# Second batch's gates, gating and out_proj placed between two layers; in_proj's weights and features split into parts

## The chip, the cores and the metric

The program runs on one core of one Trainium2 chip. The metric is device time in microseconds (us) of one execution, with all weights and activations starting in HBM. Six executions of the kernel before have a median of 670.97 us (669.88 to 676.37). One execution was profiled; it took 670.53 us, of which the profile's span covers 668.8 us.

Engine names: PE is TensorE's matmul stream (PEld its weight loads), DVE is VectorE, ACT is ScalarE, POOL is GpSimd, SP is SyncE, which here only issues DMAs. "L573" is line 573 of the kernel.

## The reference

Two fused layers on x of shape (2, 512, 256), all in fp32. Layer 0 adds to the input the product of two branches; layer 1 the same with other branches.

```
xn = layernorm(x)
s  = mamba2(xn)            # rms norm, in_proj, conv, chunked scan, silu gate, out_proj, + xn
g  = silu(moe(xn))         # 8 experts of width 704, the best 2 of each token
x  = x + s * g
xn = layernorm(x)
s  = attention(xn)         # 32 query heads, 8 key/value heads of 64, rotary, causal
g  = silu(signed_ffn(xn))  # layernorm, sign, product with the signs of the centred weights
x  = x + s * g
```

What the change touches is the end of the first branch. With `z, ssm, B, C, dt` the parts of `h @ in_proj_w` (z is the first 512 columns):

```
y_ssd = scan(conv(ssm), B, C, dt) + D * conv(ssm)
y_ssd = y_ssd * silu(z)
s     = xn + y_ssd @ out_proj_w
```

## The kernel before, in words

Tokens are cut in 8 tiles of 128 (`NT`), four per batch (`TPB`); 256 channels are `KC` = 2 contraction steps of 128. An fp32 matmul appears in the trace as two records.

**Front.** SP loads x, the small parameters and in_proj's weights `w_in` (L206, 2 DMAs). Both batches are normalised, transposed and put in `hT` (features on partitions; one tile for both batches) and `xT` (for the router). `gates(b)` (L376) computes four heads of `silu(z)` into `gT[b]` and then B and C into `BC`: each is two matmuls of 128x512 (`features`, L370). `gates(0)`, the token-major B and dt columns (L402), the router (L243 to L356), the discretisation `dt`, `la`, `cum` (L413 to L439), `convolved(0, h)` for four heads (L384) and `gates(1)` (L449) follow in the program. A framework orders each engine's instructions here by its own cost model; the result is one fixed queue per engine, executed in order.

**Experts and scan.** The mixture of experts runs as 19 blocks of 128 rows (`blocks`, `hidden` L573, `project` L588). A block's tokens and weights come by indirect DMAs on POOL (L549), its rows go back by one (L592) to the DRAM tensor `chosen`. Between the blocks stand the scan's chunks, `chunk(b, i0)` = `decays`, `outputs`, `gated`, `scanned` (L540): `gated` (L520) adds D * ssm on DVE and multiplies by `gT`; `scanned` (L532) is out_proj, four matmuls of 128x256 (L536), and the addition of `xn` into `s0` (L538). Chunks (0,0) to (0,3), (1,0) and (1,1) are complete there; of (1,2) and (1,3) only `decays`. `early_weights` (L627) loads keys' and values' weights in one tile `w_kv` (in the memory of `hT`), the rotary tables and layer 1's signed weights.

**The turn between the layers** (L907 to L932) is written in a fixed order (`manual_schedule`): SP issues the fetch of batch 0's expert rows from `chosen` (`fetched`, L681: two DMAs into `xn`, two into `y1`), then queries' weights `w_q` (2 x 1 MB), then `outputs`, `gated`, `scanned` of chunks (1,2) and (1,3). `activated` adds the two experts' rows on POOL (L694) and applies silu on ACT (L695); `residual` (L697) makes x1 and its statistics on DVE; `normed1` and `features1` normalise and transpose into `x1T`. Then come the first key, query and two value projections. `fetched(1)` overwrites `xn` rows of batch 1, so each of its DMAs must follow the `scanned` that reads those rows.

**Attention** (from L939) uses eight PSUM banks taken over from the earlier pools; its first scores (L829) can't start before the last use of the old banks, the two copies of values `v` on ACT (L780), is done. Batch 1's residual, norm and features are spread over its first steps (`others`).

Of the kernel before, what the change touches and what calls it, by code (L numbers as in the profile page):

```python
# [8 lines left out]
F32 = mybir.dt.float32  # L9
# [33 lines left out]
def fused_kernel(  # L43
# [33 lines left out]
    def bank_a():  # L77
        return psum.tile([P, 512], F32, tag="A", name="bank_a")

    def bank_b():  # L80
        return psum.tile([P, 512], F32, tag="B", name="bank_b")
# [21 lines left out]
    def par(name):  # L103
        a, w = SM[name]
        return sm[:, a : a + w]
# [66 lines left out]
    def rsqrt(var, scale, eps, name):  # L172
        return rooted(root(var, eps, name))
# [12 lines left out]
    def normed(dst, src, b, mv, r, eng=V):  # L186
        for i in range(TPB):
            t = b * TPB + i
            eng.tensor_scalar(dst[:, t, :], src[:, t, :], mv[:, i, 0:1], r[:, i : i + 1],
                              ALU.subtract, ALU.mult)  # L190
# [10 lines left out]
    def batch(b):  # L201
        return slice(b * T, (b + 1) * T)

    w_in = mem.tile([P, KC, in_w.shape[1]], F32, tag="w_in", name="w_in")
    for k in range(KC):
        nc.sync.dma_start(w_in[:, k, :], in_w[k * P : (k + 1) * P, :])  # L206
    w_out = mem.tile([P, NH, C], F32, tag="w_out", name="w_out")


# [2 lines left out]
    xn = mem.tile([P, NT, C], F32, tag="xn", name="xn")  # L212
    xT = mem.tile([P, KC, B * T], F32, tag="xT", name="xT")
    hn = mem.tile([P, NT, C], F32, tag="s0", name="hn")
    hT = mem.tile([P, KC, B * T], F32, tag="hT", name="hT")
    norms = []
    for b in range(B):
        mv, var, r = statistics(x_sb, b, "ln0")
        ms = stat.tile([P, TPB], F32, tag="ms", name=f"ms{b}")
        V.tensor_tensor(ms, r, r, ALU.mult)  # L220
        V.tensor_tensor(ms, ms, var, ALU.mult)
        rr = rsqrt(ms, 1.0, 1e-6, f"rms{b}")
        V.tensor_tensor(rr, rr, r, ALU.mult)
        norms.append((mv, r))
        normed(hn, x_sb, b, mv, rr, (V, G)[b])
        to_features(hn, b, lambda k, ps: S.mul(
            hT[:, k, batch(b)], ps, par("norm")[:, k : k + 1]))
    for b in range(B):
        normed(xn, x_sb, b, *norms[b])
        for t in range(b * TPB, (b + 1) * TPB):  # L230
# [138 lines left out]

    def features(b, col, ps):  # L370
        for k in range(KC):
            PE.matmul(ps, lhsT=w_in[:, k, col : col + P], rhs=hT[:, k, b * T : (b + 1) * T],  # L372
                      start=(k == 0), stop=(k == KC - 1))
        return ps

    def gates(b):  # L376
        for h in range(NH):
            ps = features(b, h * P, bank_a())
            S.activation(gT[b][:, h, :], ps, AF.Silu)
        for n, col in enumerate((o_b, o_c)):  # L380
            ps = features(b, col, bank_a())
            S.copy(BC[:, n, batch(b)], ps)

    def convolved(b, h):  # L384
        ps = features(b, DI + h * P, bank_b())
# [13 lines left out]
    for t in range(NT):  # L399
        ps = bank_b()  # L400
        for k in range(KC):
            PE.matmul(ps[:, : NH + P], lhsT=hT[:, k, t * P : (t + 1) * P],  # L402
                      rhs=w_in[:, k, o_dt : o_dt + NH + P],
                      start=(k == 0), stop=(k == KC - 1))
        V.tensor_tensor(dtr[:, t, :], ps[:, :NH], par("dtb"), ALU.add)
        S.copy(Btok[:, t, :], ps[:, NH : NH + P])
# [34 lines left out]
    def heads(ap):  # L441
        return ap.rearrange("p (h n) -> p h n", h=NH)

    def wide(name, t):
        return mw.tile([P, NH, P], F32, tag=name, name=f"{name}{t}")

    for h in range(NH):
        convolved(0, h)
    gates(1)  # L449


    states, parts = [None] * B, {}
# [64 lines left out]
                PE.matmul(y, lhsT=state[:, h, :], rhs=cs[:, h, :], start=False, stop=True)  # L517
        parts[t] = yps

    def gated(b, i0):  # L520

        t = b * TPB + i0
        ti = slice(i0 * P, (i0 + 1) * P)
        yps = parts[t]
        yg = wide("yg", t)
        for h in range(NH):
            V.scalar_tensor_tensor(yg[:, h, :], ssmT[b][:, h, ti], par("D")[:, h : h + 1],
                                   heads(yps)[:, h, :], ALU.mult, ALU.add)
        V.tensor_tensor(yg, yg, gT[b][:, :, ti], ALU.mult)
        parts[t] = yg  # L530

    def scanned(b, i0):  # L532
        t = b * TPB + i0
        ops = bank_b()
        for h in range(NH):
            PE.matmul(ops[:, :C], lhsT=parts[t][:, h, :], rhs=w_out[:, h, :],  # L536
                      start=(h == 0), stop=(h == NH - 1))
        V.tensor_tensor(s0[:, t, :], ops[:, :C], xn[:, t, :], ALU.add)  # L538

    def chunk(b, i0):  # L540
        for part in (decays, outputs, gated, scanned):
            part(b, i0)


# [80 lines left out]


    def early_weights():  # L627
        w_kv = mem.tile([P, 2, KC, KV * HD], F32, tag="hT", name="w_kv")
        nc.sync.dma_start(w_kv[:, 0], wk.rearrange("(k p) n -> p k n", p=P))
        nc.sync.dma_start(w_kv[:, 1], wv.rearrange("(k p) n -> p k n", p=P))  # L630
        rw = mem.tile([P, 2 * T + KC * C], F32, tag="w_in", name="rw")
        nc.sync.dma_start(rw[:, : 2 * T].rearrange("p (n t) -> p n t", n=2), rope)
        nc.sync.dma_start(rw[:, 2 * T :].rearrange("p (o c) -> p o c", o=KC),
                          ffn_w.rearrange("(o p) c -> p o c", p=P))
        return (w_kv, rw[:, : 2 * T].rearrange("p (n t) -> p n t", n=2),
                rw[:, 2 * T :].rearrange("p (o c) -> p o c", o=KC))


# [12 lines left out]
    convolved(1, 2)  # L651
    blocks(2)
    convolved(1, 3)
    w_kv, cs_t, w_f = early_weights()
    blocks(3)
    chunk(1, 0)
    blocks(5)
# [23 lines left out]
    def fetched(b):  # L681

        y1 = aw.tile([P, TPB, C], F32, tag=f"pr{b}", name=f"y1_{b}")
        by_tile = chosen.rearrange("(s p) c -> p s c", p=P)
        for t in range(b * TPB, (b + 1) * TPB, 2):
            nc.sync.dma_start(xn[:, t : t + 2, :], by_tile[:, t : t + 2, :])
            nc.sync.dma_start(y1[:, t % TPB : t % TPB + 2, :], by_tile[:, NT + t : NT + t + 2, :])
        return y1

    def activated(b, y1):  # L690

        for i in range(TPB):
            y = xn[:, b * TPB + i, :]
            G.tensor_tensor(y, y, y1[:, i, :], ALU.add)  # L694
            S.activation(y, y, AF.Silu)  # L695
# [10 lines left out]
    def means(b):  # L706
        return stat.tile([P, TPB, 2], F32, tag="mv", name=f"ln1_mv{b}")
# [1 line left out]
    x1T = mem.tile([P, KC, B * T], F32, tag="xT", name="x1T")  # L709

    def normed1(b, mv):
        var = stat.tile([P, TPB], F32, tag="var", name=f"ln1_var{b}")
        V.tensor_copy(var, mv[:, :, 1])
        normed(xn, x1, b, mv, rsqrt(var, 1.0, 1e-5, f"ln1{b}"))

    def features1(b):
        to_features(xn, b, lambda k, ps: S.copy(x1T[:, k, batch(b)], ps))
# [30 lines left out]
    def rotated(dst, ps, scale, name, between=None):  # L748

        sw = aw.tile([P, T], F32, tag="sw", name=f"sw_{name}")  # L750
        V.stream_shuffle(sw, ps, swap)
        V.scalar_tensor_tensor(dst, ps, scale, cs_t[:, 0, :], ALU.mult, ALU.mult)
        if between:
            between()
        V.scalar_tensor_tensor(sw, sw, scale, cs_t[:, 1, :], ALU.mult, ALU.mult)
        V.tensor_tensor(dst, dst, sw, ALU.add)

    def projected(w, n, b):
        ps = bank()
        for k in range(KC):  # L760
            PE.matmul(ps, lhsT=w[:, k, n * P : (n + 1) * P], rhs=x1T[:, k, batch(b)],  # L761
                      start=(k == 0), stop=(k == KC - 1))
        return ps

    kT, v_sb = {}, {}

    def key(b, m):
        if m == 0:
            kT[b] = mem.tile([P, KV // 2, T], F32, tag=f"gT{b}", name=f"kT{b}")
        rotated(kT[b][:, m, :], projected(w_kv[:, 0], m, b), HD**-0.5, f"k{b}_{m}")  # L770

    def value(b, i):
        if i == 0:
            v_sb[b] = mem.tile([P, TPB, KV * HD], F32, tag=f"ssmT{b}", name=f"v{b}")
        t = b * TPB + i
        ps = bank()
        for k in range(KC):
            PE.matmul(ps, lhsT=x1T[:, k, t * P : (t + 1) * P], rhs=w_kv[:, 1, k, :],  # L778
                      start=(k == 0), stop=(k == KC - 1))
        S.copy(v_sb[b][:, i, :], ps)  # L780

# [125 lines left out]
    with tc.manual_schedule():  # L907
        y1s = [fetched(0)]
        query_weights(0)
        query_weights(1)  # L910
        outputs(1, 2)
        gated(1, 2)
        outputs(1, 3)
        gated(1, 3)
        scanned(1, 2)

        activated(0, y1s[0])
        mvs = [means(0)]
        for t in range(2):
            residual(t, mvs[0])  # L920
        scanned(1, 3)
        y1s.append(fetched(1))
        for t in range(2, TPB):
            residual(t, mvs[0])
        normed1(0, mvs[0])
        features1(0)
        activated(1, y1s[1])
        key(0, 0)
        nextq = query(0, 0)
        for i in range(2):  # L930
            value(0, i)
        mvs.append(means(1))  # L932
# [249 lines left out]
```

## Time and profile before

| what | us |
|---|---|
| median of 6 executions | 670.97 |
| the profiled execution, whole | 670.53 |
| its span | 668.8 |
| PE busy | 624.2 |
| DVE busy | 438.3 |
| ACT busy | 376.4 |
| POOL busy | 287.9 |
| the chunks' out_proj (L536), one chunk on the chain | 1.73 to 1.76 |
| w_q (2 x 1 MB), issue to landing, median | 11.1 |
| xn and y from `chosen` (256 KB), issue to landing, medians | 3.8 and 4.0 |
| w_kv from in_wv (512 KB), issue to landing | 6.4 |

The page divides the span by engine, by 40 slices, by DMA queue, and by the chain of waits that ends with the last instruction. Busy shares are averages over stages; the stages themselves are read from tables of stretches (busy time of each engine and the TensorE clock granted, 1.00 being full speed) and from the timeline, which merges like instructions of an engine and tells, in brackets, the idle time before them and what ended it.

### The profile page before, as it was taken

The page shows a single profiled execution, that of the slowest core. Times are in us where ns is not written, and L with a number is a line of the kernel's source. Part 1 is how long each engine was busy: PE and PEld are TensorE (multiplying, and loading weights), DVE is VectorE, ACT ScalarE, POOL GpSimd, SP SyncE. Part 2 cuts the span into 40 slices and gives each one's busy share as a digit, 9 for nine tenths or more (in the row PEclk, how much of TensorE's full clock was granted, in tenths as well). Part 3 has the DMA queues.
Part 4 walks back from the last instruction along what each step waited for, and adds up shares of the span by engine and source line. Part 5 has one row for each costly group of instructions (what it writes and reads, how often), then busy time and mean ns, then how long its engine had stood idle before and what let it go on. Part 6 is the DMA issues. An engine that isn't in the chain of part 4 may idle for free.

```text
span 668.8 us, 11923 instructions
## 1 busy us (share of the span) xinstructions
PE 624.2 (93%) x4260; PEld 447.8 (67%) x4260; DVE 438.3 (66%) x1453; ACT 376.4 (56%) x948; POOL 287.9 (43%) x308
## 2 busy tenths in 40 slices
PE   1899999999999998499889999989999999999997
PEld 0564988889999987245545565546886666665676
DVE  7186856642522453689989996999228888888511
ACT  3345625522312240476888985968308988888710
POOL 2221433234455321336555746454305666677600
PEclk9999999999999999699999999999999999999999
DMA  7042140353445402500000000021000000000000
GB/s 244 9 189 95 33 152 17 131 192 120 165 159 171 151 9 80 188 1 1 1 1 1 1 1 1 2 68 60 8 25 1 1 1 1 1 2 1 1 1 32
DMA packets 17804, 38.83 MB, mean 58 GB/s; under 512 B 4845, under 2 KB 12783, under 8 KB 16592
## 3 DMA queue, kind: packets, MB, share of 16 engines
q0 software_dynamic: 7296, 24.66, 10.7%
q1 hardware_dynamic: 10448, 13.40, 6.1%
q8 instruction: 34, 0.56, 0.4%
q14 instruction: 26, 0.21, 0.1%
HBM read 56.13 MB, written 4.59 MB: 91 GB/s over the span
## 4 chain that ended last, share of the span: by engine, by line
PE 72%; DVE 17%; issue 5%; POOL 2%; DMA 2%; ACT 1%; SPq 0%; POOLq 0%; DVEq 0%
PE bank_a L573 11%; PE bank L880 9%; PE bank L888 8%; PE bank L868 7%; PE bank L761 7%; PE bank L829 7%; PE bank_a L588 6%; DVE pr L842 4%; PE bank_a L372 2%; PE bank_b L536 2%; DMA chosen<-o,dest 1%; PE bank_b L372 1%; PE bank L778 1%; PE bank L740 1%; DVE cv L394 1%
## 5 line engine op out<-in xcount | busy, mean ns | idle before, releaser
L856 POOL TENSOR_SCALAR pr<-pr,den 128x128 f32<-128x128 f32 (+2 forms) x192 | 193.4, 1023 | 159.3 <-DVE den L1039 126.1
L848 ACT ACTIVATE pr<-pr,nmax 128x128 f32<-128x128 f32 (+3 forms) x256 | 142.8, 559 | 18.6 <-DVE nmax L842 17.2
L842 DVE CUSTOM_DVE_ANT_0 pr<-bank,cmask 128x128 f32<-128x128 f32 (+3 forms) x256 | 109.8, 484 | 14.8 <-PE bank L829 14.5
L573 PEld LDWEIGHTS bank_a<-xgT,w 128*128 128x128 f32 x836 | 97.2, 192 | 2.2 <-DVE xgT L562 0.7
L573 PE MATMUL bank_a<-xgT,w 128*128 128x128 f32 x836 | 97.9, 275 | 0.5 <-DVE xgT L562 0.5
L869 ACT COPY pt<-bank 128x384 f32<-128x384 f32 (+1 forms) x192 | 85.0, 519 | 13.1 <-PE bank L868 13.1
L868 PEld LDWEIGHTS bank<-ident,pr 128*128 128x128 f32 x640 | 71.2, 141 | 24.8 <-issue 18.3
L880 PE MATMUL bank<-pt,v 128*64 128x256 f32 (+3 forms) x512 | 82.9, 443 | 0.8 <-ACT pt L869 0.8
L868 PE MATMUL bank<-ident,pr 128*128 128x128 f32 x640 | 75.7, 273 | 6.0 <-DVE oT L1023 5.7
L880 PEld LDWEIGHTS bank<-pt,v 128*64 128x64 f32 x512 | 39.2, 136 | 49.1 <-ACT pt L869 23.3
L829 PE MATMUL bank<-kT,q 64*64 64x128 f32 (+7 forms) x1024 | 69.8, 410 | 0.7 <-ACT v L780 0.7
L761 PE MATMUL bank<-x1T,w_q 128*128 128x512 f32 x124 | 61.5, 618 | 0.0
L888 PE MATMUL bank<-w_o,oT 128*128 128x256 f32 x256 | 56.1, 380 | 0.6 <-DVE oT L1020 0.6
L888 PEld LDWEIGHTS bank<-w_o,oT 128*128 128x128 f32 x256 | 48.3, 190 | 7.7 <-DVE oT L1020 0.8
L588 PE MATMUL bank_a<-wp,hid 128*128 128x256 f32 x228 | 53.4, 380 | 0.1
L549 POOL DMA_INDIRECT w<-in_moe_w,wrow x19 | 20.3, 1071 | 70.3 <-PE bank_a L560 45.8
L848 ACT ACTIVATION_READ_ACCUMULATOR pr<-pr,nmax 128x1 f32 x256 | 49.1, 192 | 0.0
L829 PEld LDWEIGHTS bank<-kT,q 64*64 64x64 f32 x1024 | 38.0, 133 | 14.3 <-issue 5.1
L577 DVE TENSOR_TENSOR hid<-hid,bank_a 128x512 f32<-128x512 f32 x19 | 13.0, 686 | 51.8 <-issue 36.6
L761 PEld LDWEIGHTS bank<-x1T,w_q 128*128 128x128 f32 x124 | 21.0, 189 | 36.9 <-issue 27.7
L588 PEld LDWEIGHTS bank_a<-wp,hid 128*128 128x128 f32 x228 | 41.4, 190 | 5.0 <-DVE hid L577 0.3
L854 ACT ACTIVATE pr<-pr,den 128x512 f32<-128x512 f32 x32 | 23.1, 723 | 22.7 <-DVE den L1061 22.7
(250 smaller groups left out, 851.7 us busy)
## 6 DMA issues: line engine op xcount, KB each, us to landing
w_q<-in_wq SPq DMA_DIRECT2D x2, 1024.0 KB, 11.1
w_o<-in_wo SPq DMA_DIRECT2D x2, 1024.0 KB, 7.2
w_in<-in_in_w SPq DMA_DIRECT2D x2, 642.0 KB, 5.9
x_sb<-in_x SPq DMA_DIRECT2D x8, 128.0 KB, 2.5
rows<-xn SPq DMA_DIRECT2D x8, 128.0 KB, 2.7
xn<-chosen SPq DMA_DIRECT2D x4, 256.0 KB, 3.8
y<-chosen SPq DMA_DIRECT2D x4, 256.0 KB, 4.0
out_x<-y SPq DMA_DIRECT2D x8, 128.0 KB, 1.7
```

What stands on the lines that cost most here:

```text
L573: PE.matmul(banks[bank][:, i * P : (i + 1) * P], lhsT=w[:, a : a + P], rhs=xgT[:, k * P : (k + 1) * P], start=(k == 0), stop=(k == KC - 1))
L588: PE.matmul(ps[:, :C], lhsT=hid[:, j * P : (j + 1) * P], rhs=wp[:, j * C : (j + 1) * C], start=(j == 0), stop=(j == 5))
L761: PE.matmul(ps, lhsT=w[:, k, n * P : (n + 1) * P], rhs=x1T[:, k, batch(b)], start=(k == 0), stop=(k == KC - 1))
L829: PE.matmul(pss[hh][to, a : a + full], lhsT=q[half, n * HD : (n + 1) * HD], rhs=kT[b][half, m, :full], start=True, stop=True)
L842: V.tensor_tensor_reduce(w["pr"][hh][:, span(i)], w["ps"][i][hh], cmask[:, i & 1, T - (i + 1) * P :], -1.0, 3.0e38, ALU.add, ALU.min, w["n ...
L848: S.activation(x, x, AF.Exp, scale=-1.0, bias=w["nmax"][hh][:, i : i + 1], accum_out=sum_of(w, i, hh))
L854: S.mul(x, x, sum_of(w, i, hh))
L856: eng.tensor_scalar(x, x, sum_of(w, i, hh), None, ALU.mult)
L868: PE.transpose(ps[:, col : col + P], pr[hh][:, at : at + P], ident)
L869: S.copy(pts[hh][:, bank_at[n] : bank_at[n] + widths[n]], ps[:, : widths[n]])
L880: PE.matmul(pv[hh * HD : (hh + 1) * HD, j * P :], lhsT=v_sb[b][:, j, g * HD : (g + 1) * HD], rhs=pts[hh][:, at : at + w], start=(j == 0), ...
L888: PE.matmul(ps[:, :C], lhsT=oTs[b][:, c, i * P : (i + 1) * P], rhs=made["w_o"][c // 8][:, c % 8, :], start=(c == 0), stop=(c == PAIRS - 1))
```

## The change

1. `w_in` is two tiles: `w_z` (the 512 columns of z) and `w_in` (the other 772), loaded by 2 + 2 DMAs. `hT` is two tiles, one for each batch.
2. `gates` takes a list of parts. In the front, `gates(1, ...)` computes only B and C. The four heads of z of batch 1 are computed in the turn.
3. `gated` is split in `passed` (D * ssm + y) and `gated` (the product with `gT`), `scanned` in `projected_out` (matmuls) and `scanned` (addition). Batch 0's chunks do all in place; batch 1's do only `passed` there, into a new tile `held` for all four chunks (in the memory of `xT`).
4. In the turn: `outputs` and `passed` of chunks (1,2), (1,3); for each head the gate's two matmuls, silu, and one product of 128x512 over all four chunks; the load of values' weights `w_v`, issued by ACT into the memory of batch 1's `hT`; `activated(0)`; four `projected_out`; four `residual`; `normed1(0)`; four `scanned`; only then `fetched(1)`.
5. `early_weights` loads keys' weights `w_k` alone, into batch 0's `hT`. The fetch of batch 0's `y1` is issued by ACT in place of SP; that of batch 1 stays with SP.
6. `normed1` reads the variances in place, without a copy.

```diff
-    w_in = mem.tile([P, KC, in_w.shape[1]], F32, tag="w_in", name="w_in")
+    w_z = mem.tile([P, KC, DI], F32, tag="w_z", name="w_z")
+    w_in = mem.tile([P, KC, in_w.shape[1] - DI], F32, tag="w_in", name="w_in")
...
-    hT = mem.tile([P, KC, B * T], F32, tag="hT", name="hT")
+    hT = [mem.tile([P, KC, T], F32, tag=f"hT{b}", name=f"hT{b}") for b in range(B)]
...
-    gates(1)
+    gates(1, range(NH, NH + 2))
...
+    def passed(b, i0):
+        t = b * TPB + i0
+        ti = slice(i0 * P, (i0 + 1) * P)
+        if b and not held:
+            held.append(mem.tile([P, NH, T], F32, tag="xT", name="held"))
+        yg = held[0][:, :, ti] if b else wide("yg", t)
+        for h in range(NH):
+            V.scalar_tensor_tensor(yg[:, h, :], ssmT[b][:, h, ti], par("D")[:, h : h + 1],
+                                   heads(parts[t])[:, h, :], ALU.mult, ALU.add)
+        parts[t] = yg
+
+    def gated(b, i0):
+        yg = parts[b * TPB + i0]
+        V.tensor_tensor(yg, yg, gT[b][:, :, i0 * P : (i0 + 1) * P], ALU.mult)
+
+    def projected_out(b, i0):
+        ops = bank_b()
+        for h in range(NH):
+            PE.matmul(ops[:, :C], lhsT=parts[b * TPB + i0][:, h, :], rhs=w_out[:, h, :],
+                      start=(h == 0), stop=(h == NH - 1))
+        parts[b * TPB + i0] = ops
 
     def scanned(b, i0):
         t = b * TPB + i0
-        ops = bank_b()
...
-        V.tensor_tensor(s0[:, t, :], ops[:, :C], xn[:, t, :], ALU.add)
+        V.tensor_tensor(s0[:, t, :], parts[t][:, :C], xn[:, t, :], ALU.add)
 
     def chunk(b, i0):
-        for part in (decays, outputs, gated, scanned):
+        for part in (decays, outputs, passed) + ((gated, projected_out, scanned) if b == 0 else ()):
             part(b, i0)
...
-            nc.sync.dma_start(y1[:, t % TPB : t % TPB + 2, :], by_tile[:, NT + t : NT + t + 2, :])
+            (nc.sync if b else nc.scalar).dma_start(y1[:, t % TPB : t % TPB + 2, :], by_tile[:, NT + t : NT + t + 2, :])
...
-        outputs(1, 2)
-        gated(1, 2)
-        outputs(1, 3)
-        gated(1, 3)
-        scanned(1, 2)
+        for i0 in (2, 3):
+            outputs(1, i0)
+            passed(1, i0)
+        for h in range(NH):
+            gates(1, (h,))
+            V.tensor_tensor(held[0][:, h, :], held[0][:, h, :], gT[1][:, h, :], ALU.mult)
+        w_v = mem.tile([P, KC, KV * HD], F32, tag="hT1", name="w_v")
+        nc.scalar.dma_start(w_v, wv.rearrange("(k p) n -> p k n", p=P))
+        late_weights.append(w_v)
 
         activated(0, y1s[0])
+        for i0 in range(TPB):
+            projected_out(1, i0)
         mvs = [means(0)]
-        for t in range(2):
-            residual(t, mvs[0])
-        scanned(1, 3)
-        y1s.append(fetched(1))
-        for t in range(2, TPB):
+        for t in range(TPB):
             residual(t, mvs[0])
         normed1(0, mvs[0])
+        for i0 in range(TPB):
+            scanned(1, i0)
+        y1s.append(fetched(1))
         features1(0)
```

## The prediction

> **What bounds the kernel now.** I read first the table of stretches, to see where PE is full. Columns: busy time (and instructions) of PE, PEld, DVE, ACT, POOL, then the granted clock, the DMA share and GB/s.
>
> ```profile
> 26.00:66.00 40.00, 39.95 (x171) 23.74 (x169) 26.61 (x118) 18.18 (x33) 6.43 (x6) 1.00 0.32 119
> 66.00:135.00 69.00, 67.37 (x440) 58.12 (x440) 45.67 (x113) 34.67 (x50) 23.93 (x22) 1.00 0.25 85
> 135.00:200.00 65.00, 65.00 (x473) 60.59 (x472) 24.37 (x55) 17.18 (x32) 29.12 (x29) 1.00 0.47 158
> ...
> 258.00:277.00 19.00, 7.74 (x49) 6.42 (x47) 12.89 (x40) 3.16 (x6) 4.03 (x5) 0.82 0.68 223
> ```
>
> Until 258 us PE has no gap worth naming; in the turn it has 11.3 us of them. So PE work taken out of a full stage pays if nothing else ends that stage, and is free in the turn if PE isn't what ends the turn. Next, what ends the turn, from the chain of waits (start, us, what):
>
> ```profile
> 257.92 4.48 DMA chosen<-o,dest
> ...
> 263.40 3.52 DMA y<-chosen
> ...
> 277.19 2.26 PE bank_a L197 x8
> ```
>
> The last expert block's rows go to DRAM, come back, and run through POOL, ACT and DVE until PE transposes them at 277.19. From there to the first scores, the timeline:
>
> ```profile
> 265.86 0.51 SPq L686 DMA_DIRECT2D xn<-chosen  x1
> ...
> 277.94 2.93 POOL L694 TENSOR_TENSOR xn<-xn,y 128x256 f32<-128x256 f32 x4 [7.72 <-DMA y<-chosen]
> ...
> 286.98 0.59 ACT L780 COPY v<-bank_b 128x512 f32<-128x512 f32 x1 [1.13 <-PE bank_b L778]
> 287.62 2.38 PE L829 MATMUL bank<-kT,q 64*64 64x128 f32 x32 [0.68 <-ACT v L780]
> ```
>
> The scores wait for the second copy of v on ACT. Ahead of that copy in ACT's queue stand batch 1's four silus, fed by POOL, fed by `fetched(1)`. Last, the places that the change empties:
>
> ```profile
> 50.47 6.17 PE L372 MATMUL bank_a<-hT,w_in 128*128 128x512 f32 x14
> 56.48 0.30 PE L437 MATMUL bank_b<-la,upper 128*128 128x32 f32 x2
> 56.62 7.11 PE L372 MATMUL bank_b<-hT,w_in 128*128 128x512 f32 x16
> ```
> ```profile
> 56.01 0.19 DVE L433 SCALAR_TENSOR_TENSOR la<-dt,ab 128x32 f32<-128x32 f32 x1
> ```
> ```profile
> 181.35 1.76 PE bank_b L536 x8
> ...
> 225.88 1.76 PE bank_b L536 x8
> ```
>
> Batch 1's gates run from 50.47 to 56.6 while DVE makes `la`, which is ready at 56.2: they fill a wait.
>
> **Front: 6.9 us of PE out, 2.0 gained.** Four heads at two matmuls of two records, 16 x 0.43 = 6.9 us. The compiled order of the changed kernel on PE tells what takes their place: after the last B/dt matmul (50.6) come three transposes of expert tokens, then `la`'s matmul (L437 before), then the convolutions. PE executes in order, so convolutions that need nothing from `la` stand behind it until 56.2, as ACT's and DVE's instructions for `la` are the same as before. PE thus idles 56.2 - 50.6 - 0.3 (transposes) = 5.3 us. The convolutions start within 0.2 us of the old time, and so does their chain (ACT copy, four DVE operations, silu: about 3.6 us a head). Behind them PE saves the last gate record pair (0.9), the transposes done early (0.3) and two waits it had (0.36 before L482, 0.48 before L573), and starts the first block's `hidden` near 64.8 instead of 67.38. Following the new DVE order by these durations, its fourth head is ready near 77.4, when PE has come to it: new waits of about 0.4. Sum: 6.9 - 5.3 - 0.4 + 0.8 = 2.0. It can't exceed 6.9 - 5.3 + 1.5 = 3.1 (all waits of that stage gone, 67.37 of 69 being busy).
>
> No row shows a gap of 5.6 us holding three transposes. The clock rows bound it:
>
> ```profile
> 270.00:270.50 0.50, 0.00 (x0) 0.00 (x0) 0.47 (x3) 0.25 (x1) 0.22 (x1) 0.66 0.91 213
> ...
> 280.00:280.50 0.50, 0.50 (x2) 0.21 (x1) 0.00 (x0) 0.48 (x2) 0.50 (x2) 0.60 0.00 0
> ```
>
> PE stopped at 265.9, the clock halved 4.3 us later (0.66 is the mean of the slice), and came back 3.1 us after work began at 277.19. A drop in the front would cost half of 3.1, 1.55, leaving 0.45. The longest stretch without any matmul is about 2.5 us (53.7 to 56.2), nearer to the gaps that cost nothing (the 4.3 before the drop), so I take no drop, and keep 0.45 as the other end.
>
> [...]
>
> **Blocks: 3.5 us.** `projected_out` of chunks (1,0) and (1,1) leaves a stage with PE 65.00 of 65.00 and 40.00 of 40.00: 2 x 1.76 = 3.5. What could be late next is a block's weights, but blocks without a chunk already run every 7.7 us without a PE wait, and those with one still take longer (2.59 of L588, 4.91 of L573, 0.2 of transposes and the chunk's remaining 2 to 3 us). DVE's two 0.69 products there cost nothing, being covered by PE.
>
> **Turn: 0.9 us longer**, on the old clock, from the same last scatter (257.92).
> - PE: `outputs` end at 261.9; gates 6.9, to 268.8; 16 out_proj matmuls (4 x 1.73 = 6.9) follow, the first 13 from 268.8 on as products arrive, done near 276.5. This fits in the 11.3 us gap; without it, 10.4 us would be on the path.
> - ACT: y1's two issues (0.4 to 0.5 each, by SP's rows) before the first silu is due at 263.6; last silu 269.4; w_v's issue, to 269.9 (its memory is free with the gates' last matmul; its 512 KB, 6.4 us by in_wv's row, are due at 283.4). Behind it stand the four silus of `activated(0)`, which began at 267.84: now 269.9, after POOL has long added.
> - DVE: four products of 0.69, paced by silu, the last to 270.1; `residual(0)` at 270.35 instead of 268.29. Four at 1.47 (271.99 to 273.46), without the old `scanned` and the slow first one (L701 0.83 against 0.43): 276.2. Root and norm 1.45 as before (L713's 0.2 is gone): transposes at 278.2, 1.0 later.
> - PE no longer cools, so the 1.55 of half clock after 277.19 is saved; values end near 286.9, as before (286.96).
> - `scanned` x4 (0.42) follow `normed1` on DVE: 279.1 to 280.8. `fetched(1)`, before at 265.86 and 272.10, now issues at 280.0 to 281.3; SP has nothing else to do until w_o's load much later. With 3.52 to land, POOL adds from 283.9 (4 x 0.73) to 286.9, ACT's last silu ends at 287.3, two copies of v at 288.45 against 287.58: +0.9. Ends: landing in 2.5 (x_sb's row) gives -0.1, since then PE's values end it; 5.4 (272.50 to 277.94) gives +2.7. I take 3.52, a fetch ahead of other traffic.
>
> **Nothing for the rest.** Two more issues on SP at 6.45 (0.48 each) end before its next job at 9.37. w_k moves from 147.93 to about 64, when the DMA share is 0.02; if it met block weights, 512 KB at the 270 to 430 GB/s that loaded stretches show would delay them 1.2 to 1.9 us. `held` takes the memory of xT, free since the router.
>
> Sum: -2.0 - 3.5 + 0.9 = -4.6 on the profiled execution: 670.53 - 4.6 = 665.9. The median shown lies 0.44 above that execution, so 666.4 for a median.
>
> **Rivals.**
> - *The clock drops in the front*: 666.4 + 1.55 = 667.9. For: idle 5.6 against 4.3. Against: transposes break it.
> - *The front gives nothing and the turn takes its upper end*: -3.5 + 2.7 + 0.44 on 670.53, 670.2. For: DVE's convolution chain is serial and now has the expert work between its steps. Against: DVE is busy 45.67 of 69 there.
> - *All moved PE work pays*: 6.9 + 3.5 - 0.9 = 9.5, 661.5. Only if PE didn't stand behind `la`; the compiled order says it does.
> - *The fetch of batch 0 is held behind w_q* (the slower side). SP now issues w_q right after two xn fetches, while y1 comes from ACT. For: the fetch issued behind w_q at 265.86 and 266.41 reached POOL only at 277.94, 11.5 us. If y1 lands with w_q, near 275, the first silu is at 275.9, `residual(0)` at 276.3 instead of 270.35: +6.0, 672.4; with POOL's pacing and the clock drop 674.5. It decides once y1 lands after 269.2. Against: y1 and w_q wait for the same event at 262.5, so y1 is issued no later.
>
> [...]
>
> **How the numbers follow.** Forecast 0.50, clock drop 0.23, nothing from the front 0.12, all pays 0.05, y1 held 0.10. Range: from 664.2 (forecast with 3.1 in the front and -0.1 in the turn, 664.3) to 669.4, which covers the drop (667.9) with most of the turn's upper end; outside are "all pays", "y1 held" and part of the third. A measurement of this kernel can tell about 0.5% from no change, 3.35 us: below 667.6 is faster, above 674.3 slower. Faster: 0.44 of the forecast's 0.50, 0.08 of the drop, 0.05: 0.57. Slower: 0.07, mostly from y1. Same: 0.36.
>
> **What would show it.** Right: PE idle from about 50.7 to 56.2 with `la`'s matmul at its end; the chain of the blocks' end 5 to 6 us earlier; no drop of the clock in the turn; scores about 30.5 us after the last scatter's issue (29.7 before), waiting for v's copies on ACT. Wrong: `hidden` of the first block not before 66; clock 0.5 near 57; POOL's first add later than 11 us after the last scatter.

## The result, and the profile after

The changed kernel takes 675.09 us (median of 35 runs, 673.71 to 678.08); the kernel before, run beside it, 672.22. The ratio is 1.0043 with a 95% interval of 1.0034 to 1.0053: slower by some 2.9 us, where 4.6 us of gain were forecast, and outside the range given. The execution profiled took 673.78 us, with a span of 672.1 (before 668.8); it is one of the fastest, 1.3 us below the median, and no execution of it on record was granted a higher clock than its 0.990.

Four marks split the span. "Forecast" is the mark that the prediction's own steps give for the profiled execution.

| mark, us | before | forecast | after |
|---|---|---|---|
| first block's `hidden` starts on PE | 67.38 | 64.8 | 67.80 |
| last scatter to `chosen` issued | 257.92 | 252.4 | 260.27 |
| first scores | 287.62 | 283.0 | 291.27 |
| end of span | 668.8 | 664.2 | 672.1 |

So, for the profiled execution, 3.0 us are missing by the first block, 4.9 more in the blocks and 0.4 in the turn; what follows takes as long as before (380.8 us from the scores on, 381.2 before). The table of stretches of the changed kernel shows the first two places. The columns are stretch, length, busy time (and instructions) of PE, PEld, DVE, ACT, POOL, then the granted clock, the DMA share and GB/s.

```profile
26.00:66.00 40.00, 35.00 (x150) 21.23 (x149) 24.21 (x114) 15.65 (x29) 7.44 (x7) 0.91 0.34 122
66.00:135.00 69.00, 64.25 (x416) 55.71 (x415) 46.48 (x111) 36.38 (x50) 20.93 (x19) 0.98 0.24 80
135.00:200.00 65.00, 65.00 (x461) 59.60 (x460) 24.40 (x56) 18.16 (x32) 28.57 (x28) 1.00 0.45 150
...
57.00:62.00 5.00, 5.00 (x7) 2.18 (x8) 1.85 (x5) 0.59 (x1) 0.00 (x0) 0.50 0.08 32
129.70:134.00 4.30, 4.30 (x16) 3.78 (x17) 1.38 (x5) 0.51 (x2) 0.13 (x1) 0.60 0.82 328
...
281.00:285.00 4.00, 4.00 (x12) 2.43 (x12) 1.97 (x6) 1.24 (x3) 0.00 (x0) 0.63 0.41 127
```

PE now has 5.0 us of gaps in 26 to 66 and 4.75 in 66 to 135 (0.05 and 1.63 before). In three places PE works at half clock, each right behind a gap. The timeline of the front (start, length, engine, line, operation; in brackets the idle time before it and what ended it):

```profile
53.02 0.44 PE L577 MATMUL bank_a<-ident,xg 128*128 128x128 f32 x2 [2.14 <-DMA xg<-rows,tok]
55.07 0.33 PE L577 MATMUL bank_a<-ident,xg 128*128 128x128 f32 x1 [1.61 <-DMA xg<-rows,tok]
56.60 0.61 PE L443 MATMUL bank_b<-la,upper 128*128 128x32 f32 x2 [1.20 <-DVE la L439]
57.02 9.65 PE L377 MATMUL bank_b<-hT,w_in 128*128 128x512 f32 x16
```

PE idles 2.14 + 1.61 + 1.20 = 4.95 us until `la`, as forecast (5.3). But the 16 records of the convolutions take 9.65 us in place of 7.11: 2.5 us lost to the clock (0.50 in 57 to 62). In finer slices the half clock reaches from 55.3 to 62.1.

The second place, in the timeline around the two waits of the blocks (L605 is `project`, L594 the product that makes `hid`, L476 to L496 the scan's `decays`):

```profile
108.95 0.38 PE L577 MATMUL bank_a<-ident,xg 128*128 128x128 f32 x2
109.04 0.86 DVE L476 SCALAR_TENSOR_TENSOR L<-bank_b,cum,negm 128x128 f32<-128x128 f32 x3
...
109.82 0.15 DVE L480 TENSOR_TENSOR dte<-bank_b,cum 128x4 f32<-128x4 f32 x1
109.89 0.68 DVE L496 TENSOR_TENSOR cs<-BC,ec 128x512 f32<-128x512 f32 x1
110.48 0.68 DVE L594 TENSOR_TENSOR hid<-hid,bank_a 128x512 f32<-128x512 f32 x1
...
111.27 1.10 PE L605 MATMUL bank_a<-wp,hid 128*128 128x256 f32 x4 [1.93 <-issue]
...
127.43 0.86 DVE L476 SCALAR_TENSOR_TENSOR L<-bank_b,cum,negm 128x128 f32<-128x128 f32 x3
...
128.27 0.69 DVE L496 TENSOR_TENSOR cs<-BC,ec 128x512 f32<-128x512 f32 x1
...
128.87 0.69 DVE L594 TENSOR_TENSOR hid<-hid,bank_a 128x512 f32<-128x512 f32 x1
...
129.66 0.67 PE L605 MATMUL bank_a<-wp,hid 128*128 128x256 f32 x2 [2.83 <-issue]
```

DVE has no gap in either. It works through five operations of the next chunk's `decays` (L476 three times, L480 and L496), and only then makes the product for which PE stands still. ACT isn't what the product waits for: the silu that it reads (L593) was done at 101.7 and 119.2. At the same place the kernel before had put a chunk's `outputs` between the block's `hidden` and its `project`, and PE waited 0.69 us (the same view of before):

```profile
108.61 0.38 PE L560 MATMUL bank_a<-ident,xg 128*128 128x128 f32 x2
...
109.69 1.12 PE L502 MATMUL bank_b<-xe,Btok 128*128 128x512 f32 x2 [0.69 <-DVE xe L492]
...
110.35 0.69 DVE L577 TENSOR_TENSOR hid<-hid,bank_a 128x512 f32<-128x512 f32 x1 [0.38 <-ACT hid L576]
...
112.43 0.81 PE L588 MATMUL bank_a<-wp,hid 128*128 128x256 f32 x3
```

The turn after, from the chain of waits (start, us, what); its lines of before stand in the prediction:

```profile
264.25 6.88 PE bank_a L377 x16
271.15 0.41 ACT gT L385
...
272.40 0.43 DVE xn L716
...
280.78 2.25 PE bank_a L197 x8
...
290.26 0.97 ACT v L794 x2
291.27 2.38 PE bank L843 x32
```

The gates, the last silu and four residuals now set the transposes at 280.78, 20.5 us after the last scatter (issued at 260.27; 19.3 before); the scores follow it by 31.0 (29.7 before, 30.6 forecast). What they wait for is what was forecast, the copies of v behind batch 1's silus on ACT; POOL stood idle for 1.28 us before its second pair of additions for them (at 288.40), and the last silu ended 30.0 us after the scatter, where 29.4 were worked out.

### The profile page after: what moved, and what is told of

Same layout as the page of the kernel before. It is cut to its first block, busy times and chain, and to the rows that moved or that the text cites. A ratio compares the mean times of both kernels' runs of the same rounds, so it can differ in the third digit from the quotient of the medians.

```text
span 672.1 us, 11934 instructions
## 1 busy us (share of the span) xinstructions
PE 628.4 (94%) x4260; PEld 450.2 (67%) x4260; DVE 439.2 (65%) x1452; ACT 379.7 (56%) x950; POOL 288.3 (43%) x308
## 4 chain that ended last, share of the span: by engine, by line
PE 44%; DVE 14%; issue 1%; POOL 1%; ACT 0%; DVEq 0%; POOLq 0%; ACTq 0%
PE bank L894 9%; PE bank L902 8%; PE bank L882 7%; PE bank L775 7%; PE bank L843 7%; DVE pr L856 4%; PE bank L792 1%; PE bank L754 1%; PE bank_a L377 1%; DVE sw_q L765 1%; DVE xn L189 1%; DVE q L766 1%; POOL pr L870 1%; DVE oT L1042 1%; DVE oT L1039 1%
## 5 line engine op out<-in xcount | busy, mean ns | idle before, releaser
L856 DVE CUSTOM_DVE_ANT_0 pr<-bank,cmask 128x128 f32<-128x128 f32 (+3 forms) x256 | 109.9, 485 | 14.2 <-PE bank L843 14.1
L894 PE MATMUL bank<-pt,v 128*64 128x128 f32 (+3 forms) x512 | 82.9, 443 | 0.8 <-ACT pt L883 0.8
L605 PE MATMUL bank_a<-wp,hid 128*128 128x256 f32 x228 | 54.6, 386 | 4.8 <-issue 4.8
L902 PE MATMUL bank<-w_o,oT 128*128 128x256 f32 x256 | 56.1, 380 | 0.6 <-DVE oT L1039 0.6
L605 PEld LDWEIGHTS bank_a<-wp,hid 128*128 128x128 f32 x228 | 41.9, 193 | 10.0 <-issue 5.2
L594 DVE TENSOR_TENSOR hid<-hid,bank_a 128x512 f32<-128x512 f32 x19 | 13.1, 687 | 52.7 <-issue 36.6
```

Of the source, the lines that this page charges most:

```text
L605: PE.matmul(ps[:, :C], lhsT=hid[:, j * P : (j + 1) * P], rhs=wp[:, j * C : (j + 1) * C], start=(j == 0), stop=(j == 5))
L856: V.tensor_tensor_reduce(w["pr"][hh][:, span(i)], w["ps"][i][hh], cmask[:, i & 1, T - (i + 1) * P :], -1.0, 3.0e38, ALU.add, ALU.min, w["n ...
L894: PE.matmul(pv[hh * HD : (hh + 1) * HD, j * P :], lhsT=v_sb[b][:, j, g * HD : (g + 1) * HD], rhs=pts[hh][:, at : at + w], start=(j == 0), ...
L902: PE.matmul(ps[:, :C], lhsT=oTs[b][:, c, i * P : (i + 1) * P], rhs=made["w_o"][c // 8][:, c % 8, :], start=(c == 0), stop=(c == PAIRS - 1))
```

## The experiments

All twelve, in one table; the marks are those of each profiled execution.

| run | median us | ratio to before, 95% | last scatter | scores |
|---|---|---|---|---|
| changed kernel | 675.09 | 1.0043 (1.0034 to 1.0053) | 260.27 | 291.27 |
| e1_gates_front | 668.54 | 0.9942 (0.9922 to 0.9962) | 254.68 | 284.93 |
| e2_hid_first | 669.06 | 0.9952 (0.9932 to 0.9972) | 255.53 | 287.38 |
| e3_conv_first | 667.55 | 0.9917 (0.9891 to 0.9944) | 254.00 | 285.73 |
| e4_conv_hid | 663.07 | 0.9850 (0.9825 to 0.9875) | 251.77 | 283.11 |
| e5_filler | 671.97 | 0.9992 (0.9974 to 1.0009) | 258.14 | 289.31 |
| e6_wq_late | 663.30 | 0.9865 (0.9843 to 0.9886) | 248.22 | 280.55 |
| e7_turn | 661.10 | 0.9832 (0.9809 to 0.9854) | 248.66 | 278.49 |
| e8_before_hid | 674.44 | 1.0043 (1.0020 to 1.0067) | 260.25 | 291.40 |
| e9_filler2 | 674.75 | 1.0036 (1.0024 to 1.0048) | 260.65 | 292.18 |
| e10_before_conv_hid | 673.83 | 1.0026 (1.0010 to 1.0041) | 260.17 | 291.55 |
| e11_filler_hid | 667.19 | 0.9927 (0.9906 to 0.9949) | 253.38 | 285.42 |
| e12_turn_only | 672.91 | 1.0006 (0.9990 to 1.0022) | 261.48 | 292.42 |

**e1: one part undone.** In the changed kernel, batch 1's z gates go back to the front.

```diff
-    gates(1, range(NH, NH + 2))
+    gates(1)
...
-            gates(1, (h,))
```

> The changed kernel with one part undone: the four z heads of batch 1 are computed in the front again (gates(1) whole), and the turn only multiplies. Its compiled order in front and blocks is that of the kernel before, less the two out_proj. Theory (the loss sits in the order of the fixed queues: PE idle ahead of la's matmul with a half clock behind it, and two waits of 1.93 and 2.83 us ahead of project's matmuls with another half clock): hidden of the first block starts near 67.4, no wait ahead of project, the last scatter is issued near 257.9 - 3.5 = 254.4, no half clock before the turn; time 672.2 - 3.5 + 0 to 1.3 for the turn = 668.7 to 670.0. Rival (taking out_proj out of the blocks frees nothing, or the split of weights and features costs time by itself): last scatter near 257.9 or later, 672 to 674.

The stretch of the blocks' first part, and the last scatter in the timeline:

```profile
66.00:135.00 69.00, 67.37 (x441) 57.99 (x440) 45.88 (x115) 34.77 (x49) 23.85 (x22) 1.00 0.26 89
```
```profile
254.68 0.98 POOL L609 DMA_INDIRECT chosen<-o,dest  x1 [6.50 <-ACTq L686]
```

Measured: `hidden` at 67.67, no wait ahead of `project`, the last scatter at 254.68 (3.24 before that of the kernel before), 668.54 us. The out_proj taken from the blocks does come through there (3.24 of 3.5), and the split of weights and features costs nothing that shows. Moving the z gates as well is what turns this gain into a loss.

**e2: the product first.** The framework orders by the program's sequence and its own cost model; `high_priority` lets `hid`'s five instructions (two silus on ACT, three products on DVE) count as written earlier.

```diff
+        with tc.high_priority(400):
             S.activation(hid[:, : 4 * P], banks[0], AF.Silu)
             V.tensor_tensor(hid[:, : 4 * P], hid[:, : 4 * P], banks[1], ALU.mult)
...
```

> The changed kernel with the two silus and three products that make hid put ahead of the scan's operations in ACT's and DVE's queues; no work is moved or left out. Theory (DVE held the product behind the scan's operations, and that wait is what PE stood in): the waits of 1.93 and 2.83 us ahead of project and the half clock of 130.4 to 133.8 (1.7) are gone, the front is as in the changed kernel (hidden near 67.8); last scatter near 260.3 - 6 = 254, time 675.1 - 4.8 to 6.5 = 668.6 to 670.3. Rival (project waits for its weights or for ACT's table loads): the waits stay, 674 to 676.

Measured: 669.06 us. The table of stretches of e2 shows a full PE in the blocks and the same front as the changed kernel:

```profile
26.00:66.00 40.00, 35.02 (x150) 21.29 (x149) 24.00 (x113) 15.40 (x28) 7.42 (x7) 0.91 0.33 122
66.00:135.00 69.00, 69.00 (x459) 60.05 (x458) 47.72 (x113) 42.77 (x57) 23.78 (x22) 1.00 0.28 91
```

Both waits and the half clock behind the second are gone (69.00 of 69.00 busy at 1.00 in 66 to 135) with no work taken out or added, so the order of the queues made them; that it was DVE's rather than ACT's follows from the trace above, where the silu had long been done. The last scatter comes 4.7 us earlier, not 6: `hidden` started 0.3 later in this execution, and a new wait of 0.82 stands at 246.

**e3 and e4: work for PE while `la` is made.** The convolutions' matmuls are issued ahead of `la`'s; e4 is e3 with e2's edit.

```diff
+    for h in range(4):
+        multiplied(0, h)
     ps = bank_b()
     PE.matmul(ps[:, : NT * NH], lhsT=upper, rhs=la.rearrange("p t h -> p (t h)"),
```

(`multiplied` is the first line of `convolved`, the matmuls into a bank; `convolved` then goes on from that bank.)

> The changed kernel with the matmuls of batch 0's convolutions issued before la's matmul, so that PE has work while DVE makes la. Theory: no idle of 4.9 us and no half clock from 55.3 to 62.1; la comes some 3 us later as DVE runs the first convolution between its steps; hidden of the first block starts near 60 in place of 67.8. Were the blocks as in the changed kernel that would be 667; their order is new here, so 664 to 670. Rival (the convolutions' chain on ACT and DVE ends the front, not PE): hidden starts early but the blocks then wait by as much, 673 to 676.

> e3 and e2 together. Theory: hidden of the first block near 60 and no wait above 1 us ahead of project, no half clock between 26 us and the turn: last scatter near 247 to 250, time 661 to 665. Rival (weights of the blocks become the bound once the blocks start earlier, or DVE does): last scatter 252 or later, 667 or more.

The front of e3, in its timeline:

```profile
51.49 7.03 PE L377 MATMUL bank_b<-hT,w_in 128*128 128x512 f32 x16
58.35 0.60 PE L586 MATMUL bank_a<-ident,xg 128*128 128x128 f32 x4
59.39 0.38 PE L452 MATMUL bank_b<-la,upper 128*128 128x32 f32 x2 [0.44 <-DVE la L446]
59.63 1.60 PE L599 MATMUL bank_a<-xgT,w 128*128 128x128 f32 x12
...
69.99 0.33 PE L498 MATMUL bank_b<-ident,ssmT 128*128 128x128 f32 x1 [3.47 <-ACT ssmT L408]
```

`hidden` starts at 59.63 in place of 67.80, and the convolutions take 7.03 us, at a clock of 1.00 from 26 to 66; a later wait of 3.47 for a convolved head gives part of it back, as the rival said, but only part: 667.55 us. The two waits ahead of `project` (1.93 and 2.83) aren't in this trace, though nothing was edited there: the compiled order of the blocks changed again with this edit, so e3 is no measure of the front alone. With `hid` ahead the wait of 3.47 is gone, and e4 takes 663.07. Its profiled execution took 666.07: the clock was halved in the router's stage there (0.57 in 30 to 38, where before, the changed kernel, e2 and e3 show 1.00), and `hidden` started at 62.68. Its marks in the table are late by that. In the 4 us before the slice of the fall (0.56 in 30 to 32) PE shows no gap (4.00 of 4.00); from 27.04 to 32.0 it has the router's matmuls of 128x8 but for 1.10 us. That these caused it isn't shown.

**e5 and e9: the gap filled with matmuls that nobody reads**, to tell the idle time from the clock behind it.

```diff
+    spare = bank_b()
+    for i in range(5):
+        PE.matmul(spare, lhsT=w_z[:, 0, :P], rhs=hT[1][:, 0, :], start=True, stop=True)
     ps = bank_b()
     PE.matmul(ps[:, : NT * NH], lhsT=upper, rhs=la.rearrange("p t h -> p (t h)"),
```

(e9 has `range(2)`.)

> The changed kernel with five matmuls of 128x512 whose results nobody reads, put on PE between the last B/dt matmul and la's matmul; the rest of each engine's order stays as it was, but for one transpose and one matmul of the first hidden that stand ahead of la. Theory (the idle time itself costs nothing, as la sets the start, but the half clock from 55.3 to 62.1 behind it costs 2.5): clock 1.00 throughout the front, la's matmul still near 56.6, convolutions in 7.1 in place of 9.65, hidden of the first block near 65.2, the same two waits ahead of project, last scatter near 257.8, time 675.1 - 2.5 = 672.6. Rival (the convolutions' chain on DVE and ACT sets hidden, not the clock): hidden near 67.8, 674.5 to 676.

> As e5, with two unread matmuls in place of five: PE is idle for about 3.2 us in pieces between the last B/dt matmul and la's matmul, in place of 1 (e5) or 4.9 (changed kernel). If the clock goes by the busy share of a stretch of some 3.4 us (1.93 us idle kept it, 2.4 and 2.8 didn't), the pieces matter by where they fall: clock kept, and 672 as e5, if no such stretch is more than about two thirds idle; else the half clock and 674.5 to 675.5. The two fillers stand at the front of the gap, so the stretch that ends at 55.3 is about 60% idle: I expect it kept, with little certainty.

The timelines of the front, e5 and then e9:

```profile
51.40 4.45 PE L444 MATMUL bank_b<-hT,w_z 128*128 128x512 f32 x10
...
57.62 0.31 PE L446 MATMUL bank_b<-la,upper 128*128 128x32 f32 x2
57.77 7.11 PE L377 MATMUL bank_b<-hT,w_in 128*128 128x512 f32 x16
...
65.90 4.41 PE L593 MATMUL bank_a<-xgT,w 128*128 128x128 f32 x38
```
```profile
55.36 0.44 PE L580 MATMUL bank_a<-ident,xg 128*128 128x128 f32 x2 [1.79 <-DMA xg<-rows,tok]
...
57.58 9.80 PE L377 MATMUL bank_b<-hT,w_in 128*128 128x512 f32 x16
...
68.41 4.41 PE L593 MATMUL bank_a<-xgT,w 128*128 128x128 f32 x38
```

With five, more than four microseconds of useless work make the kernel 3.1 us faster (671.97): the clock stays (1.00 from 50.5 to 65), the convolutions take 7.11, and `hidden` starts at 65.90 (two of its records, and one transpose, now stand ahead of `la`) although `la`'s matmul is 1 us later than in the changed kernel. By the marks of the profiled executions the gain is 1.9 us at `hidden` and 2.1 at the last scatter. The two waits ahead of `project` stand unchanged (1.93 and 2.83). With two, my guess that the clock would be kept was wrong: both ran at the start of the gap, from 52.7 to 56.1 PE worked for 0.88 us, the clock fell at 56.2 and stayed at 0.50 to 63.0, the convolutions took 9.80, and nothing was gained.

**e11: both effects taken away, nothing moved** (e5's filler and e2's `high_priority`).

> The changed kernel with both omitted effects taken away and nothing moved: five unread matmuls in the front's gap (e5) and hid ahead of the scan's operations (e2). Theory (two effects make up what the forecast lacked): the two gains add up, 675.1 - 3.1 - 6.0 = 666.0, with 665 to 667.5; last scatter near 253.5. Rival (they overlap, or a third loss is left): 668 or more.

The table of stretches shows the clock kept in the front and a full PE in the blocks:

```profile
26.00:66.00 40.00, 38.95 (x171) 23.69 (x171) 25.38 (x116) 17.59 (x30) 8.92 (x8) 1.00 0.34 126
66.00:135.00 69.00, 69.00 (x468) 60.91 (x467) 47.05 (x112) 41.77 (x57) 23.07 (x22) 1.00 0.30 99
```

Measured: 667.19 us, last scatter at 253.38. The two nearly add up (7.9 us of 9.1), and the time lies 0.8 us above the forecast of 666.4. Against the kernel before run beside it (672.38) the gain is 5.2 us, where 4.6 were forecast.

**e8 and e10: the same reordering without the change.** e8 is the kernel before with e2's edit, e10 the kernel before with e4's.

> The kernel before (no part of the change), with hid's silus and products put ahead as in e2. Theory (the gain of e2 to e4 is the moved work coming through, not the order itself: PE of the kernel before has no gap of more than 0.7 us from 67 us to 258): the waits of 0.48 and 0.69 can go, 671 to 672.5. Rival (the order alone is worth 5 us in any kernel): 667 or less.

> The kernel before with the convolutions' matmuls ahead of la's as in e4 and hid ahead. Theory: batch 1's gates stand behind the convolutions then, PE is as full as before, and all waits of 26 to 135 us together (1.7) are the most that can be gained: 670 to 672.5, some 8 us above e4. Rival (the order is the gain): 666 or less.

Measured: 674.44 and 673.83, slower than the kernel before by 0.43% and 0.26%, and 1.9 and 1.3 us above the ranges expected. PE has as little idle time in 66 to 135 as before (67.17 and 67.42 of 69 busy), with waits in other places. By the marks, the profiled executions lose 0.8 and 1.1 us by the first block, 1.5 and 1.2 in the blocks, and 1.5 and 1.7 in the turn, where the mean clock from 260 to 292 is 0.79 in both: some 13.4 us of half clock by an estimate from that mean (0.21 x 32 / 0.5), in place of 10.2 (0.84). So the order by itself is worth nothing; it lets the moved work come through, some 11 us between e4 and these two.

**e6, e7, e12: the turn.** e6 is e4 with `w_q` issued by ACT after the second gate's silu. e7 goes on from there; e12 is e7's turn alone in the changed kernel. The order of e7's turn:

```diff
-        for h in range(NH):
+        for h in range(3):
             gates(1, (h,))
-            V.tensor_tensor(held[0][:, h, :], held[0][:, h, :], gT[1][:, h, :], ALU.mult)
+            gating(h)
+            if h == 1:
+                query_weights(0)
+                query_weights(1)
+        activated(0, y1s[0], (0,))
+        gates(1, (3,))
...
+        activated(0, y1s[0], (1, 2, 3))
+        residual(0, mvs[0])
+        gating(3)
         for i0 in range(TPB):
             projected_out(1, i0)
...
+        activated(1, y1s[1], (0, 1))
         key(0, 0)
         nextq = query(0, 0)
         for i in range(2):
             value(0, i)
+        activated(1, y1s[1], (2, 3))
```

> e4 with the two loads of w_q issued by ACT after the second gate's silu, about 2.5 us later than SP does, so that batch 0's second pair of fetches has the DMA engines to itself. Theory (y's second pair, added by POOL only 9.4 us after its issue, is slowed by w_q): POOL adds the second pair right after the first, 2 to 3.5 us earlier; but DVE's chain of four residuals waits only 0.6 for it, so the time falls by 0.2 to 0.7, to 662.4 to 662.9. Rival (w_q comes too late for the query at 277): query's matmuls wait, 664 or more.

> e6 and a new order in the turn: batch 0's first silu and residual stand ahead of the fourth gate's silu and product, and the last two silus of batch 1 behind the copies of v on ACT. Theory (the turn is set by the chain add, silu, four residuals on DVE, norm, transposes; the changed kernel starts it 12.1 us after the last scatter because ACT and DVE do the fourth gate first): first residual 10.3 to 10.9 us after the last scatter, transposes 1.3 to 2 earlier, no half clock behind them (up to 1.5 more), scores 28.5 to 30 us after the scatter in place of 31.3: time 660.3 to 662. Rival (out_proj, held back by the fourth product, ends the turn, or the clock still drops): 662.5 to 664.

> The changed kernel with the new order of the turn of e7 alone; front and blocks stay as in the changed kernel. Theory (what e7 gained on e4 belongs to the turn, whatever stands before it): last scatter near 260.3 as in the changed kernel, no half clock in the turn, scores 29.8 us after the scatter in place of 31.0: 675.1 - 1.2 to 2.0 = 673.1 to 673.9. Rival (the turn's gain needs the blocks' new order): 674.5 or more.

In e6 POOL adds all four tiles in one go (x4 from 257.66, no wait for the second pair of `y`, where e4 has one of 3.45), so `w_q` did slow that pair; yet the time is that of e4 (663.30 and 663.07, intervals overlapping). DVE's chain had waited only 0.6 for the pair, and batch 1's first addition came 27.1 us after the last scatter in place of 25.9; why it did was not followed. In e7 the first residual starts 10.65 us after the last scatter in place of 12.1, PE's gap ahead of the transposes is 0.45 us, and the clock holds through the turn (1.00 in 260 to 292), as its timeline and its stretch show:

```profile
259.31 0.93 DVE L726 TENSOR_TENSOR xn<-xn,s 128x256 f32<-128x256 f32 x1
...
262.43 5.88 PE L558 MATMUL bank_b<-w_out,held 128*128 128x256 f32 x26 [1.62 <-DVE held L939]
...
268.75 1.69 PE L197 MATMUL bank_a<-ident,xn 128*128 128x128 f32 x8 [0.45 <-issue]
```
```profile
260.00:292.00 32.00, 29.02 (x152) 16.31 (x151) 27.08 (x86) 19.48 (x50) 11.47 (x12) 1.00 0.29 97
```

661.10 us, 1.7% below the kernel before: the best version here. In e12 the median falls by 2.2 us against the changed kernel, a little more than expected. Its trace doesn't show where from: the execution profiled took 674.91, the slowest of the twelve, a gap of 1.96 us stood within out_proj, the clock was halved from 275.6 to 279.1, and the scores followed the scatter by 30.9, as in the changed kernel. Over whole executions the granted clock was 0.991 or 0.992 in nine of e12's twelve, 0.986 in the one profiled, and never above 0.990 in the changed kernel: most executions of e12 hold less half clock, but where isn't recorded. So that the turn gave the 2.2 us is argued from the medians alone, and how often its clock falls stays open.

## Why the prediction was wrong

**"Front: 6.9 us of PE out, 2.0 gained"** failed at one term. The order (convolutions behind `la`), the idle time (4.95 us, 5.3 forecast) and the start of the convolutions (57.02, 0.4 later than before) were right or nearly so. Of the two ends for the clock, "I take no drop" was the wrong one: three small transposes in the gap did not keep the clock (0.83 in 54 to 56, 0.50 in 56 to 62), and the half clock cost 2.5 us, more than the 1.55 of the other end. That end was mis-sized too: the half clock of the kernel before lasts 10.2 us (270.2 to 280.4) in all, and the 3.1 us after PE's start were only what was left of it; here it lasted 6.8. e5 shows the clock as a cause, since keeping it, with one transpose and two records of `hidden` moved, gave 3.1 us. The rival named for this, the clock drop, was true; with it alone the forecast would have been 667.9. The drop was set aside for a row (4.3 us from the stop of PE to the drop) that doesn't say how long a gap may be, only how long it took in that one case.

**"Blocks: 3.5 us"** is where most is missing. The size is right (e1: 3.24), but the sentence on what could be late next looked at weights and at DVE's busy share, and took the order of the blocks for unchanged. In the changed kernel's compiled order it is not: `project` follows `hidden` directly where `outputs` stood between, and on DVE the product stands behind the scan. The two waits (4.76) and half a clock over 3.4 us behind the second (1.7) make 6.5; less 0.94 of idle time that the kernel before had in that stretch and 0.4 that the forecast allowed for new waits, 5.1, against 4.9 missing. So the step that failed is the term for new waits in the blocks, put at nothing beyond those 0.4. e2 and e11 show the cause. The prediction followed DVE's new order through the front only; the same order, followed to 130 us, holds both waits.

**"Turn: 0.9 us longer"** was 1.3. The gates, products, first residual (12.1 us after the scatter; forecast 12.4 by the same count from 257.92 to 270.35) and out_proj came as worked out. "PE no longer cools" was wrong: out_proj ended at 278.4, 2.4 us before the transposes (the prediction's own times left 1.7 there, 276.5 to 278.2), and the clock fell again (280.6 to 284.0). The 1.55 to be saved there was not. The path that was taken to end the turn, `fetched(1)`, silus, copies of v, was right.

**The rivals.** "The front gives nothing" happened, for the clock's reason rather than DVE's. "All moved PE work pays" was set aside since the compiled order forbade it; true of that order, but e3 shows that moving one loop gives it back. "The fetch of batch 0 is held behind w_q" was false: POOL's first add came 9.1 us after the scatter, within the bound of 11. Only the second pair of fetches was slowed, and the time didn't hang on it (e6). None of the rivals had the blocks' order in it, so the range could not hold what came.

**"Nothing for the rest"** held: the loads in parts and the earlier `w_k` show in no stretch, and e1 has both.

## What to carry to other kernels

When a framework orders the queues by its own cost model, taking work out of one place reorders others: compare the compiled order of each engine over the whole stretch, not only where the edit stands, and look for a product that PE waits for behind independent work. Gaps of a few microseconds on PE can cost twice: here 4.95 us of them in the front, and 2.5 more by the half clock behind them. So independent matmuls belong there: with the convolutions (e3) or five unread matmuls (e5) in those gaps the clock stayed at 1.00. A change that moves work from a full stage to an empty one can lose although its idea is right: here the same moves end at 661.1 us with edits of order alone.

## What the hardware showed that was not expected

In these traces the half clock came in whole steps. In the changed kernel it holds from 55.3 to 62.1, from 130.4 to 133.8 and from 280.6 to 284.0: 6.8, 3.4 and 3.4 us. By the mean clock of the slices at its ends (0.99 in 130.2 to 130.4, 0.98 in 133.8 to 134.0) the second lasts 3.41. The falls are 75.1 and 150.2 us apart, 22 and 44 steps of 3.41. Fine slices of other traces show half clock for 10.2 us (before, 270.2 to 280.4), 3.4 (e5, 128.7 to 132.1), 6.8 (e9, 56.2 to 63.0) and twice 3.4 (e12, 111.8 to 115.2 and 275.6 to 279.1, the falls 163.8 apart, 48 steps): all eight last one, two or three such steps.

The length of a gap alone did not tell here whether the clock falls. The wait of 1.93 us ahead of `project` at 109.3 left the clock alone (1.00 in every slice from 108 to 114), and so did the same wait in e5 (1.00 from 108 to 113.2); behind the same wait in e12 the clock was halved:

```profile
110.84 2.83 PE L605 MATMUL bank_a<-wp,hid 128*128 128x256 f32 x8 [1.93 <-issue]
```

Eight records take 2.83 us there (1.97 in the changed kernel), and the slices show half clock from 111.8 to 115.2. In e12 the wait lies within the 3.41 us before the fall. In the changed kernel, by steps counted back from 130.4 (an estimate), a step ends at 109.9, within the wait, and leaves 1.35 us of it behind that point. That this place made the difference is argued from these two cases alone, and that the busy share of a step decides, as the expectation of e9 supposed, isn't shown. No threshold follows: a gap of 1.82 us ahead of out_proj in e1 (at 260.48) left its 32 records at 0.24 us each, as long as the 6 records ahead of the gap of 1.96 in e12; the 26 behind that gap took 0.29 each, and the clock fell there. Executions of one kernel differ with the clock granted: those of the changed kernel at 0.990 took 673.7 to 675.0 us, those at 0.984 took 677.0 and more. Where their gaps and falls lie isn't recorded, so what makes this difference isn't shown.
